# A two-layer decoder on one core: router by column tiles, two sequences in shared parts, and another order

## The chip, the core and the metric

The kernel runs on one core of a Trainium2 chip. Such a core has TensorE (matmuls and transposes, writing to PSUM), VectorE, ScalarE and GpSimd for the elementwise work, and SyncE, which issues nearly all transfers here; the five run side by side and meet at semaphores. The metric is the device time of one execution, in microseconds (us). Profiles name the engines PE, DVE, ACT, POOL and SP; PEld is TensorE's loading of weights.

## What is computed

Sixteen sequences of 128 tokens with 256 features go through six residual blocks, all in f32, with a context of the same shape for the two cross attentions:

```python
x = x + L0_attn(layernorm(x), qk, ov)                  # causal, one head of 256
x = x + L0_xattn(layernorm(x), ctx, ctx, mask, ...)    # 16 heads of 16
x = x + L0_ffn(layernorm(x), ...)                      # 1024 hidden, 4 of 16 blocks of 64 chosen by a router
x = x + L1_attn(layernorm(x), ...)                     # 16 heads, adds its own normalised input too
x = x + L1_xattn(layernorm(x), ctx, ctx, cell, ...)    # own layer norms, rotation, causal, equal cells
x = x + L1_ffn(layernorm(x), ...)                      # 8 experts of 128, the best 2, and a shared one of 256
```

The block FFN takes `softmax(x @ w_router + b_router)` and keeps a hidden block where it is among the four best. The expert FFN takes `sigmoid(x @ gate.T)`, keeps the two best experts, divides their scores by their sum and multiplies by 2.5:

```python
shared_out = swiglu(x, ws_gate, ws_up, ws_down)
topk_w, topk_idx = top_k(sigmoid(x @ gate_weight.T), 2)
combine = einsum("tk,tke->te", 2.5 * topk_w / (topk_w.sum(-1, keepdims=True) + 1e-20), one_hot(topk_idx, 8))
y = einsum("tei,ehi->teh", silu(g) * u, w_down)        # g, u: of every expert
out = einsum("te,teh->th", combine, y) + shared_out
```

## The kernel before

**Lanes.** Two sequences make a lane (`G = 2`, 256 tokens), so there are eight lanes (`NL`), whose x stays on the chip from the first load to the output. All work is written for one lane at a time. The expert FFN is dense: every lane goes through all eight experts, and a token's share of an expert it did not choose is zero.

**Steps of a lane.** `layer_0` (L1107) runs `causal_attention` (L677), `context_attention` (L730) and `block_ffn` (L762); `layer_1` (L1116) runs `self_attention` (L820) and `windowed_attention` (L855); `expert_ffn` (L964) follows by itself. Each normalises x (L343), transposes it on TensorE (`transposed`, L386, giving `srcT` with the tag `xT`) and multiplies. `attention` (L486) handles one sequence: scores for 16 heads in two score tiles (tag `s`, four PSUM banks), VectorE's row maxima `top`, a transpose `topT`, the maxima subtracted in `qs` on GpSimd, the scores once more the other way round, the exponentials `p` on ScalarE, and the products with the values `oT`, which use column tiles of the array: four tiles of 128 rows by 32 columns that work side by side. The scores use four row tiles of 32 rows. `unseen` holds masks, added to the scores by small bf16 matmuls (`hide`, L475).

**The parts that the change touches.** `router` (L621) multiplies with x as the stationary side and the router's 16 or 8 columns moving, for each sequence and half of the features; the logits stand in PSUM token by token, and for layer 0 VectorE adds the bias row. `values` (L441) projects one sequence into a bank, and VectorE adds the bias into the value tile `v`, then the other. `causal_attention` runs values, scores, softmax, transpose and product once for each sequence (`one`, L686). The sums of both FFNs (`y`) are made one sequence at a time, each in a bank of its own and added to x by VectorE. GpSimd adds the row biases to x, one sequence at a time. `rotate` (L652) fetches swapped rows through SyncE into the buffer `swap`, and GpSimd and VectorE combine them.

**The order.** It is written out by a planner, `Turns` (L65 to L240), at build time. The steps are generators; each `yield` names the engine of the next piece and the buffers it takes (`dict(bank=1)`), and `give` returns them. The planner keeps a time for each engine and each buffer from its own costs. `run` (L211) takes, among all threads whose buffers are there, the piece that can begin first, and among equals the one of lowest rank; the instructions of each engine are issued in that order, and nothing is reordered on the chip. A piece is never broken. `LIMITS` (L334) holds the number of buffers of each tag; `bank` are the four PSUM banks beside the scores'. Five lanes are in work at a time (`IN_FLIGHT`, L1121): layer 0 of lanes 0 to 7, then layer 1 of lanes 0 to 7, each begun when an earlier one ends (`more`, L1123). The expert weights come into the place of the block FFN's once the last layer 0 has ended (`late_weights`, L1096), and an expert FFN begins when a layer 1 is done, at most three beyond those ended.

Of the kernel before, what the change touches and what calls it, by code (L numbers as in the profile page):

```python
# [32 lines left out]


# [9 lines left out]
C_ALL = C_TRI8 + NE * NE  # L44
# [6 lines left out]
    ("L1_xattn_b_q", 2), ("L1_xattn_b_k", 2),  # L51
# [3 lines left out]
    ("L1_xattn_b_v", D), ("L1_xattn_b_o", D), ("L0_ffn_b_router", NB),  # L55
# [19 lines left out]

class Turns:
# [5 lines left out]

    HOP = 70.0
    HOP_FROM_PE = 200.0
    SWITCH = 91.0

# [21 lines left out]
    def give(self, tag, n=1):  # L108
        self.tiles[tag] += [self.now.at] * n
# [27 lines left out]
    def act(self, name, out, *args, **kw):  # L137
        self.charge(ACT, 200 + 0.8 * self.width(out, args))
        getattr(self.nc.scalar, name)(out, *args, **kw)  # L139
# [7 lines left out]
    def moved(self, n_bytes):  # L147

        self.moves = max(self.moves, self.now.at) + n_bytes / 300.0
        self.now.at = self.moves + 2000.0  # L150

# [59 lines left out]
    def run(self, more):  # L211

        while True:
            more()
            best = None
            for i, th in enumerate(self.threads):
# [13 lines left out]
                if ok and (best is None or (at, th.rank, i) < best[0]):  # L230
                    best = (at, th.rank, i), th
# [3 lines left out]
            (at, _, _), th = best  # L235
# [4 lines left out]
            th.at, th.last = max(th.at, at), engine  # L240
            self.resume(th, None)


class Thread:
    def __init__(self, gen, rank, at, parent):
        self.gen, self.rank, self.at, self.parent = gen, rank, at, parent
        self.last, self.ask, self.waits, self.children, self.result = None, None, 0, [], None
# [3 lines left out]
def decoder(ctx: ExitStack, tc: tile.TileContext, a: dict, out: bass.AP):  # L251
# [6 lines left out]
    ps_s = ctx.enter_context(tc.tile_pool(name="ps_s", bufs=2, space=PSUM))  # L258
    ps = ctx.enter_context(tc.tile_pool(name="ps", bufs=4, space=PSUM))

    dram = ctx.enter_context(tc.tile_pool(name="dram", bufs=1, space=bass.MemoryType.DRAM))
# [54 lines left out]

    scaled_bias = {
# [7 lines left out]
    v_tiles = [keep.tile([P, G, H * HA + CT - HA], F32, name=f"v{i}") for i in range(4)]  # L325
# [4 lines left out]
    for t in tops:  # L330
        nc.gpsimd.memset(t, 0.0)


    LIMITS = dict(  # L334
        bank=4, s=2, oT=1, xn=6, xT=5, qk=5, qs=3, kb=3, v=4, p=4, oS=2, on=4, hm=8, tmp=3, rank=2, selT=2, p0=2,
        pT0=2, unseen=4, chosen=3, swap=2, words=1, top=3,
# [77 lines left out]
    def project(w, at, xT, j):  # L414

        q.landed(w)
        t = bank([P, D], "pr")
        for d in range(DC):
            q.matmul(t, xT[:, d, j * S : (j + 1) * S], w[:, d, at : at + D], start=d == 0, stop=d == DC - 1)
        return t  # L420

# [19 lines left out]
    def values(w, at, xT, bias):  # L441
        yield PE, dict(v=1, bank=1)
        v = v_tiles.pop(0)
        for j in range(G):
            if j:
                yield PE, dict(bank=1)
            t = project(w, at, xT, j)
            yield DVE
            q.dve(
                "tensor_tensor",  # L450
                v[:, j, 0 : H * HA].rearrange("p (h e) -> p h e", e=HA)[:, :, 0:HD],
                t.rearrange("p (h e) -> p h e", e=HD),
                row(bias).rearrange("p (h e) -> p h e", e=HD),
                ALU.add,
            )
            q.give("bank")
        return v
# [28 lines left out]
    def attention(qT, kb, v, j, unseen=None, to=None):  # L486
# [7 lines left out]
        yield PE, dict(s=2)  # L494
        ss = banks()
# [11 lines left out]
        for t2, s in enumerate(ss):  # L507
# [4 lines left out]
            q.give("s")  # L512
        yield PE, dict(bank=1)
# [16 lines left out]
        yield PE, dict(s=2)  # L530
        ss = banks()
# [12 lines left out]
        def exponentials(s):  # L544
# [3 lines left out]
            q.give("s")  # L548
            return p

        pTs = yield [exponentials(s) for s in ss]
        yield PE, dict(oT=1, bank=1)

# [17 lines left out]
        q.give("bank")  # L571
        yield PE, dict(bank=1)
# [48 lines left out]
    def router(w, xT, n):  # L621
        yield PE, dict(bank=1)
        t = bank([P, G, n], "rt")
        for j in range(G):
            for d in range(DC):
                q.matmul(t[:, j, :], xT[:, d, j * S : (j + 1) * S], w[:, d, :], start=d == 0, stop=d == DC - 1)
        return t

    def output_projection(on, w, l, j, gain=None, bias=None, free=None):
# [16 lines left out]
        y = project(w, 0, oT, 0)  # L646
# [30 lines left out]
    def causal_attention(l):  # L677
# [8 lines left out]
        def one(j):  # L686
            js = slice(j * S, (j + 1) * S)
            yield PE, dict(bank=1)
            t = project(w["ov"], 0, xT, j)
            yield ACT, dict(on=1)  # L690
            v = new("on", [P, D], "v1")
            q.act("copy", v, t)
            q.give("bank")
            yield PE, dict(bank=1)
            s = bank([P, S], "s0")
            for d in range(DC):
                q.matmul(s, qT[:, d, js], xT[:, d, js], start=d == 0, stop=d == DC - 1)
            yield DVE, dict(p0=1)
            p = new("p0", [P, S], "p0")
            q.dve("tensor_tensor", p, s, causal, ALU.add)  # L700
            q.give("bank")
            m = small.tile([P, 1], F32, tag="m0", name="m0")
            q.dve("tensor_reduce", m, p, AX.X, ALU.max, negate=True)
            yield ACT
            total = small.tile([P, 1], F32, tag="total", name="total")
            q.act("activation", p, p, AF.Exp, bias=m, accum_out=total)
            yield PE, dict(bank=1)
            t = bank([P, S], "pt0")
            q.transpose(t, p, ident)
            q.give("p0")  # L710
            yield ACT, dict(pT0=1)
            pT = new("pT0", [P, S], "pT0")
            q.act("copy", pT, t)
            q.give("bank")
            yield PE, dict(bank=1)
            o = bank([P, D], "o0")
            q.matmul(o, pT, v, start=True, stop=True)
            q.give("pT0")
            q.give("on")
            yield DVE  # L720
            r = small.tile([P, 1], F32, tag="r0", name="r0")
            q.dve("reciprocal", r, total)
            q.dve("scalar_tensor_tensor", x[l][:, j, :], o, r, x[l][:, j, :], ALU.mult, ALU.add)
            q.give("bank")

        yield [one(j) for j in range(G)]
        q.give("xT")
        q.give("qk")

# [32 lines left out]
    def block_ffn(l):  # L762

        xT = yield from transposed((yield from normalise(x[l])))
        rt = yield from router(w["r0"], xT, NB)
        yield DVE, dict(chosen=1)
        pr = small.tile([P, G, NB], F32, tag="pr", name="pr")
        q.dve("tensor_tensor", pr, rt, row("L0_ffn_b_router").unsqueeze(1).to_broadcast([P, G, NB]), ALU.add)
# [15 lines left out]
        for j in range(G):  # L784
            q.pool("tensor_tensor", x[l][:, j, :], x[l][:, j, :], row("L0_ffn_b2"), ALU.add)
# [21 lines left out]
        for j in range(G):  # L807
            yield PE, dict(bank=1)
            y = bank([P, D], "y0")
            for f in range(8):  # L810
                q.matmul(
                    y, hm[f // 2][:, f % 2, j * S : (j + 1) * S], w["w2"][:, f, :], start=f == 0, stop=f == 7
                )
            if j == G - 1:
                q.give("hm", 4)
            yield DVE
            q.dve("tensor_tensor", x[l][:, j, :], x[l][:, j, :], y, ALU.add)
            q.give("bank")

    def self_attention(l):  # L820
# [4 lines left out]
        def residual():  # L825
            for j in range(G):

                yield POOL
# [408 lines left out]
```

## Time and profile before

| what | us |
|---|---|
| median of three runs | 850.48 (850.39 to 851.54) |
| the profiled execution | 849.42 |
| its span, first to last instruction | 847.4 |
| router matmuls, 128, by their records | 16.0 |
| `v` bias adds, VectorE, 48 | 20.1 (0.418 each) |
| `x<-x,y` adds, VectorE, 32 | 13.4 (0.418 each) |
| `x<-x,rows` adds, GpSimd, 32 | 23.6 (0.751 each) |

An f32 matmul appears as two matmul instructions. Matmuls are pipelined: a record of 0.38 us can be followed by the next start after 0.22. So a group's busy time is the union of its records, and what an instruction holds the array is read from the distance of two starts. The 40 slices of the span show who is busy when, in tenths:

```
PE   6999999999999999999979999999999999999998
DVE  5446565565262644546685686675566575555533
ACT  4555434362544354626747565565343424212111
POOL 5345454153165443636777875445422331100000
```

The one slice of TensorE below nine in the middle is the 21st, from 424 to 445 us. In the last nine slices ScalarE and GpSimd have little to do: only expert FFNs are left.

### The profile page before, as it was taken

Reading aid. Unit: us, or ns where it says so; the run is one execution under the profiler, and the core shown is the slowest. Engines: PE = TensorE matmul, PEld = TensorE weight load, DVE = VectorE, ACT = ScalarE, POOL = GpSimd, SP = SyncE. Lnnn points to the kernel's source line nnn. Section 1 sums busy time; section 2 is a strip of 40 time slices with the busy share of each in tenths; the row PEclk is TensorE's granted clock in tenths of the full one; section 3 lists DMA queues with packets and bytes.
Section 4 is the critical chain, followed back from the end, with each engine's and each line's share of the span. In section 5 each row is a group of like instructions: output and inputs, shape, how many; then the busy total and the mean of one; then the engine's idle time right before and its main releaser. Section 6 shows DMA issues by size and latency. Waiting matters only on the chain.

```text
span 847.4 us, 19890 instructions
## 1 busy us (share of the span) xinstructions
PE 818.3 (97%) x8128; PEld 661.2 (78%) x8128; DVE 481.7 (57%) x1218; ACT 372.1 (44%) x801; POOL 350.0 (41%) x606
## 2 busy tenths in 40 slices
PE   6999999999999999999979999999999999999998
PEld 5877678778787777876758867878778888888887
DVE  5446565565262644546685686675566575555533
ACT  4555434362544354626747565565343424212111
POOL 5345454153165443636777875445422331100000
PEclk9999999999999999999999999999999999999999
DMA  8325202112100000160120102010100100000000
GB/s 285 113 72 162 70 25 34 36 38 78 40 1 13 2 2 2 39 187 1 52 64 13 53 3 74 3 48 30 51 2 1 63 13 2 13 1 14 13 12 13
DMA packets 41178, 36.83 MB, mean 43 GB/s; under 512 B 6784, under 2 KB 36608, under 8 KB 40448
## 3 DMA queue, kind: packets, MB, share of 16 engines
q1 hardware_dynamic: 41088, 35.57, 13.8%
q8 instruction: 64, 1.05, 0.5%
q14 instruction: 26, 0.21, 0.1%
HBM read 27.16 MB, written 4.19 MB: 37 GB/s over the span
## 4 chain that ended last, share of the span: by engine, by line
PE 85%; DVE 6%; POOL 4%; ACT 2%; issue 2%; DMA 1%; SPq 0%; POOLq 0%; ACTq 0%; DVEq 0%
PE gu L126 16%; PE s L126 14%; PE y L126 14%; PE pj L126 11%; PE pr L126 9%; PE hp L126 7%; PE oT L126 5%; PE tps L131 3%; PE o L131 2%; PE rt L126 2%; DVE top L135 1%; POOL rstd L145 1%; DMA swap<-kT 1%; ACT p L139 1%; PE wb L126 1%
## 5 line engine op out<-in xcount | busy, mean ns | idle before, releaser
L135 DVE TENSOR_REDUCE top<-s 128x8 f32<-128x1024 f32 x96 | 112.8, 1217 | 31.1 <-PE s L126 31.0
L139 ACT ACTIVATE p<-s 128x1024 f32<-128x1024 f32 x96 | 94.6, 1027 | 60.0 <-PE s L126 60.0
L126 PE MATMUL gu<-srcT,gu 128*128 128x256 f32 x512 | 118.4, 380 | 1.5 <-DVE hm L135 0.9
L145 POOL TENSOR_TENSOR qs<-qT,less 128x512 f32<-128x512 f32 x48 | 61.0, 1272 | 112.1 <-ACT less L139 105.7
L126 PEld LDWEIGHTS gu<-srcT,gu 128*128 128x128 f32 x512 | 93.8, 190 | 16.8 <-DVE hm L135 1.2
L139 ACT ACTIVATE sg<-gu 128x256 f32<-128x256 f32 x80 | 30.8, 385 | 116.6 <-PE gu L126 111.2
L145 POOL TENSOR_SCALAR rstd<-mv 128x2 f32<-128x2 f32 x72 | 16.6, 230 | 121.0 <-DVE mv L135 116.6
L126 PE MATMUL hp<-srcT,L_w 128*128 128x256 f32 x256 | 65.9, 387 | 0.0
L126 PE MATMUL s<-qs,kb 32*128 32x128 f32 x1536 | 59.4, 286 | 5.7 <-POOL qs L145 2.9
L126 PEld LDWEIGHTS s<-qs,kb 32*128 32x128 f32 x1536 | 49.5, 188 | 16.9 <-issue 7.3
L126 PE MATMUL y<-L_w,hm 128*128 128x256 f32 x256 | 59.0, 383 | 0.0
L126 PE MATMUL y<-down,hm 128*128 128x256 f32 x256 | 58.4, 381 | 0.0
L145 POOL TENSOR_SCALAR kb<-kT,consts 128x256 f32<-128x256 f32 x96 | 53.1, 566 | 10.3 <-ACT kT L139 9.7
L126 PE MATMUL s<-kb,qT 32*128 32x256 f32 x768 | 56.5, 401 | 0.6 <-DVE top L135 0.6
L126 PE MATMUL oT<-p,v 128*32 128x128 f32 x1536 | 52.5, 276 | 2.1 <-ACT p L139 2.0
L135 DVE TENSOR_TENSOR x<-x,y 128x256 f32<-128x256 f32 x32 | 13.4, 418 | 71.4 <-PE y L126 71.4
L126 PEld LDWEIGHTS y<-L_w,hm 128*128 128x128 f32 x256 | 47.7, 190 | 8.0 <-issue 1.5
L145 POOL TENSOR_TENSOR rstd<-rstd,power 128x2 f32<-128x2 f32 x72 | 51.3, 713 | 6.0
L126 PEld LDWEIGHTS hp<-srcT,L_w 128*128 128x128 f32 x256 | 44.3, 190 | 11.5 <-issue 3.3
L126 PEld LDWEIGHTS y<-down,hm 128*128 128x128 f32 x256 | 47.8, 190 | 6.3 <-issue 0.2
L145 POOL TENSOR_TENSOR eq<-eq,consts 128x512 bf16<-128x512 bf16 (+1 forms) x16 | 15.0, 940 | 89.7 <-DVE eq L135 89.6
L135 DVE SCALAR_TENSOR_TENSOR sg<-sg,gu 128x256 f32<-128x256 f32 x80 | 33.2, 415 | 31.3 <-ACT sg L139 31.1
(149 smaller groups left out, 1625.1 us busy)
## 6 DMA issues: line engine op xcount, KB each, us to landing
unseen<-hidden SPq DMA_DIRECT2D x128, 64.0 KB, 2.4
c<-in_ctx SPq DMA_DIRECT2D x16, 256.0 KB, 3.0
x<-in_x SPq DMA_DIRECT2D x8, 256.0 KB, 6.3
L_w<-in_L_w SPq DMA_DIRECT2D x2, 1024.0 KB, 6.4
hidden<-plain SPq DMA_DIRECT2D x32, 64.0 KB, 1.5
gu<-in_L_gu SPq DMA_DIRECT2D x2, 1024.0 KB, 5.2
swap<-kT SPq DMA_DIRECT2D x16, 128.0 KB, 2.1
swap<-qT SPq DMA_DIRECT2D x16, 128.0 KB, 2.1
```

Source lines behind the costliest of these rows:

```text
L126: self.nc.tensor.matmul(out, lhsT, rhs, **kw)
L131: self.nc.tensor.transpose(out, src, ident)
L135: getattr(self.nc.vector, name)(out, *args, **kw)
L139: getattr(self.nc.scalar, name)(out, *args, **kw)
L145: getattr(self.nc.gpsimd, name)(out, *args, **kw)
```

## The change

The file also gets code that sorts tokens by expert and runs only the chosen ones (`routing`, `shared`, `plan`, `expert_tile`, `combining`, `blank`). It is reached for lanes named in `GROUPS`, and that is empty, so all lanes take `expert_ffn` as before; of that code there remain a few small constant tables (33 more columns of `consts`, two 128x128 tiles made once by VectorE).

The router makes four products, one for each sequence and half of the features, in the four column tiles, with the router's columns padded to 32 as the stationary side and x moving. ScalarE copies the result (with the bias, in layer 0), TensorE transposes it once, and VectorE adds the two halves:

```diff
+    def router(w, xT, n, bias=None):
         yield PE, dict(bank=1)
-        t = bank([P, G, n], "rt")
+        t = bank([P, S], "rT")
         for j in range(G):
             for d in range(DC):
-                q.matmul(t[:, j, :], xT[:, d, j * S : (j + 1) * S], w[:, d, :], start=d == 0, stop=d == DC - 1)
-        return t
+                c = j * DC + d
+                q.matmul(
+                    t[c * CT : (c + 1) * CT, :], w[:, d, :], xT[:, d, j * S : (j + 1) * S], start=True, stop=True
+                )
+        yield ACT, dict(p0=1)
+        sb = new("p0", [P, S], "rT")
+        if bias is None:
+            q.act("copy", sb, t)
+        else:
+            q.act("activation", sb, t, AF.Identity, bias=col(bias, 0))
+        q.give("bank")
+        yield PE, dict(bank=1)
+        t = bank([P, G * DC, CT], "rt")
+        q.transpose(t.rearrange("p c n -> p (c n)"), sb, ident)
+        q.give("p0")
+        return t.rearrange("p (g d) n -> p g n d", d=DC)[:, :, 0:n]
...
-        q.dve("tensor_tensor", pr, rt, row("L0_ffn_b_router").unsqueeze(1).to_broadcast([P, G, NB]), ALU.add)
+        q.dve("tensor_reduce", pr, rt, AX.X, ALU.add)
...
-        yield ACT
-        sc = small.tile([P, G, NE], F32, tag="sc", name="sc")
-        q.act("activation", sc, rt, AF.Exp, scale=-1.0)
-        q.give("bank")
+        yield DVE
+        sc = small.tile([P, G, NE], F32, tag="sc", name="sc")
+        q.dve("tensor_reduce", sc, rt, AX.X, ALU.add)
+        q.give("bank")
+        yield ACT
+        q.act("activation", sc, sc, AF.Exp, scale=-1.0)
```

`values`, the FFN sums and causal attention put both sequences into one bank, and one instruction of VectorE or ScalarE takes them out; in causal attention the exponentials and the last scaling stay one for each sequence. GpSimd's bias adds cover both sequences too.

```diff
+    def products(parts):
+        y = bank([P, G, D], "y")
+        for j in range(G):
+            pairs = parts(slice(j * S, (j + 1) * S))
+            for i, (a, b) in enumerate(pairs):
+                q.matmul(y[:, j], a, b, start=i == 0, stop=i == len(pairs) - 1)
+        return y
...
-        for j in range(G):
-            yield PE, dict(bank=1)
-            y = bank([P, D], "y0")
...
-            yield DVE
-            q.dve("tensor_tensor", x[l][:, j, :], x[l][:, j, :], y, ALU.add)
-            q.give("bank")
+        yield PE, dict(bank=1)
+        y = products(lambda js: [(hm[f // 2][:, f % 2, js], w["w2"][:, f, :]) for f in range(8)])
+        q.give("hm", 4)
+        yield DVE
+        q.dve("tensor_tensor", x[l], x[l], y, ALU.add)
+        q.give("bank")
```

The order: a thread that holds score tiles, or asks for them, is treated as if it could begin 200 ns earlier; `holds` is set ahead of each pass over the scores and cleared after the maxima, and after the copy `oS`. The planner's cost of a ScalarE instruction with a bias or scale of its own per row grows by 80 ns each. The turns and buffers change, and the limit of three on begun experts goes:

```diff
+    LEAD = 200.0
...
-                if ok and (best is None or (at, th.rank, i) < best[0]):
-                    best = (at, th.rank, i), th
+                first = th.holds or "s" in takes
+                key = (max(at - self.LEAD * first, self.free_at[engine] - first), not first, th.rank, i)
+                if ok and (best is None or key < best[0]):
+                    best = key, th, at
...
-        bank=4, s=2, oT=1, xn=6, xT=5, qk=5, qs=3, kb=3, v=4, p=4, oS=2, on=4, hm=8, tmp=3, rank=2, selT=2, p0=2,
-        pT0=2, unseen=4, chosen=3, swap=2, words=1, top=3,
+        bank=4, s=2, oT=1, xn=6, xT=4, qk=5, qs=3, kb=3, v=3, p=4, oS=2, on=4, xe=1, hm=8, tmp=3,
+        rank=2, selT=2, p0=2, pT0=1, unseen=4, chosen=3, swap=1, words=1, top=3,
...
+    TURN = [(0, l) for l in range(7)]
+    for l in range(NL):
+        TURN += [(1, l), (0, l + 7)] if l + 7 < NL else [(1, l)]
...
-        if n < 2 * NL and n - len(ended) < IN_FLIGHT and (n < NL or n - NL in ended[:NL]):
+        if n < 2 * NL and n - len(ended) < IN_FLIGHT and (TURN[n][0] == 0 or (0, TURN[n][1]) in ended):
...
-        if ready and experts_begun[0] < min(len(ended) - NL, experts_ended[0] + 3):
-            l = ended[NL + experts_begun[0]]
+        dense = [l for k, l in ended if k and l not in group_of]
+        if ready and experts_begun[0] < len(dense):
+            l = dense[experts_begun[0]]
```

So the turns are layer 0 of lanes 0 to 6, layer 1 of lane 0, layer 0 of lane 7, layer 1 of lanes 1 to 7.

## The prediction

> **What bounds the kernel now.** I read the page first: who is busy, and what the chain of waits runs through.
>
> ```profile
> PE 818.3 (97%) x8128; PEld 661.2 (78%) x8128; DVE 481.7 (57%) x1218; ACT 372.1 (44%) x801; POOL 350.0 (41%) x606
> ...
> PE 85%; DVE 6%; POOL 4%; ACT 2%; issue 2%; DMA 1%; SPq 0%; POOLq 0%; ACTq 0%; DVEq 0%
> ```
>
> TensorE is busy in 97% of the span and carries 85% of the chain; nobody else is above 57%. So a step counts here only if it takes TensorE's time, or makes TensorE wait. A matmul's recorded end is modelled, so I used its starts instead: from one instruction's start to the next.
>
> ```profile
> 103.86 0.96 PE L126 MATMUL rt<-L_router,srcT 128*128 128x16 f32 x8
> 104.67 0.63 PE L131 MATMUL o<-consts,oS 128*128 128x128 f32 x4
> ...
> 100.80 1.08 PE L126 MATMUL oT<-p,v 128*32 128x128 f32 x32
> 101.81 0.48 PE L126 MATMUL hp<-srcT,L_w 128*128 128x256 f32 x1
> ```
>
> In the timeline of TensorE (start, length, and how many), a router's eight instructions hold the array from 103.86 to 104.67, 0.81 us; the 32 column-tiled ones of one attention from 100.80 to 101.81, 1.01 us. (An f32 matmul is two instructions, so the counts are twice the matmuls of the code.) Taking every kind at its usual distance (0.216 us for 128x256 f32, 0.109 for a transpose and so on) and adding up all 8128, TensorE needs 761 us of work. It changes between whole-array and tiled shapes 330 times; each costs 0.09 us, seen as 1.82 us in place of 1.73 for eight projection instructions that a tiled one follows: 30 us. It first starts at 6.2 us, and 3.8 us come after its last start. 847.4 - 761 - 30 - 6.2 - 3.8 leaves 46 us of real waits. That is all that an order can win.
>
> Where they lie, by the view of stretches (time, TensorE busy):
>
> ```profile
> 100.00:350.00 250.00, 247.03 (x2455) 198.62 (x2454) 129.32 (x308) 109.64 (x238) 108.54 (x174) 1.00 0.09 23
> 350.00:525.00 175.00, 164.87 (x2131) 129.17 (x2130) 112.02 (x260) 103.95 (x210) 113.04 (x191) 0.99 0.19 57
> 425.00:450.00 25.00, 19.64 (x314) 14.56 (x312) 18.64 (x39) 13.39 (x27) 19.07 (x28) 0.93 0.17 50
> 525.00:665.00 140.00, 137.67 (x1550) 110.23 (x1549) 87.63 (x216) 69.04 (x143) 57.73 (x98) 1.00 0.08 24
> 665.00:844.00 179.00, 178.37 (x1074) 151.35 (x1072) 97.30 (x287) 37.73 (x94) 20.99 (x38) 1.00 0.04 14
> ```
>
> By starts, the 46 us are: 9.5 up to 100 us (loads and a cold pipeline), 9.6 from 100 to 350, 19.9 from 350 to 525, 5 from 525 to 665, 2 after that. The thick part is 350 to 525, and its reason is in the lists of FFN and expert work: the last block-FFN sum ends at 366.0, the first expert matmul is this:
>
> ```profile
> 522.49 1.03 PE L126 MATMUL pr<-L_qkv,srcT 128*128 128x256 f32 x4
> 523.35 1.03 PE L126 MATMUL gu<-srcT,gu 128*128 128x256 f32 x4
> ```
>
> For 157 us there is only attention, whose chain goes over five engines, and no long FFN work to put between. After 665 us there is nothing to win: experts run back to back.
>
> **The router** (L621). Removed: eight instructions, 0.81 us. Added: eight of the column-tiled form, a quarter of the attention's (1.01 less the way out of the tiled shape, 0.13, is 0.88; a quarter 0.22), 0.09 into the tiled shape, 0.13 out, and one transpose of 0.11: 0.55. Saved 0.26 in each of 16 routers: 4.2 us. Bounds: a router that lies beside other tiled work pays no change of shape (0.33, saved 7.7); one whose transpose finds its copy late pays a start of 0.1 more (saved 2.6). Beside it ScalarE gets 16 copies (0.46 by the row of a 128x128 activation with a column bias, 0.28 by that of a plain copy: 5.9 us in all), and VectorE eight small reductions more (0.18 by `mr`, 1.5 us); the other eight stand for the bias add of 0.19. Both engines have over 40% free, so nothing on the path. The router itself answers some 1 us later (copy, two hops, transpose); the other four lanes hide this, and in the tail a router runs one expert ahead (that at 728.29 belongs to the expert whose matmuls start near 761.8). Behind the waiting copy stand other lanes' exponentials, which give the score banks back; a copy that finds its matmuls late holds them by the 0.2 us of a hop. Without cover it is 16 x 1 = 16 us. The wider router tables add under 0.1 MB of loads, behind which only later lanes' x wait: nothing.
>
> **Shared parts.** TensorE's matmuls stay the same in number and size in values (L441), causal attention (L677) and both sums. What changes is the pieces: values lose 24 of 48, causal attention 32 of 64, the sums 16 of 32, 72 pieces fewer, each of which could find its semaphore late. Pieces of kind `pr` have 6.4 us of waits in 78 groups, 0.08 each; for 72 pieces that would be 5.9, yet most of it lies in a few long waits that stay. I take 2 us, bounds 0 and 5.9. VectorE's adds become half as many: 0.42 for 256 columns, 0.68 (the shortest 128x512 row, `swap`) to 0.85 (its mean) for 512; GpSimd's bias adds 0.75 against 1.27. Both engines gain a little, which is off the path, but at the very end it is not:
>
> ```profile
> 842.88 1.03 PE L126 MATMUL y<-L_shared,hm 128*128 128x256 f32 x4
> 843.95 0.42 DVE L135 TENSOR_TENSOR x<-x,y 128x256 f32<-128x256 f32 x1 [3.90 <-PE y L126]
> 844.40 0.37 SPq L1035 DMA_DIRECT2D out_x<-x  x1
> ```
>
> The last add is now of 512 columns: 0.3 us later (0.26 to 0.43). What stands behind it is the output's DMA alone.
>
> [...] Today the first sequence's add at 839.63 runs while TensorE sums the second in another bank. [...]
>
> **The order.** Four things in it. (a) Layer 1 of lane 0 is begun before layer 0 of lane 7. Begins follow ends, and the ends stand one turn apart (sums end at 205.4 and 237.2), so layer 1 begins some 32 us earlier, and the last block FFN ends as much later: the stage without FFN shrinks from 157 to about 93 us. Its waits above the rate of 100 to 350 (1 us in 25) are 19.9 - 7 = 12.9; times 93/157 is 7.6: saved 5 us. Bounds: nothing, and all 12.9. (b) Threads that hold a score bank go first, and TensorE may be kept free up to 0.2 us for them. That is at most 144 pieces x 0.2 = 29 us of new waits, and at most the 16 us that now lie ahead of scores, masks and values on TensorE as a gain; the first needs every piece to use its whole lead, so I take 0 with bounds -10 and +10. (c) Fewer buffers: xT 5 to 4, v 4 to 3, swap 2 to 1. One swap buffer was held from its DMA at 423.45 to the GpSimd add's end at 438.9, 15.4 us; sixteen of these are 246 us in the 313 from 367 to 680. One buffer is just enough, so rotations will queue; SyncE has `unseen` and `c` loads behind them, and attention waits for these. I take 2 us, bounds 0 and 19 (below). (d) The limit on experts begun falls; `hm` holds one at a time anyway (5 of 8): nothing.
>
> **The sum.** -4.2 - 2 + 0.3 - 5 + 0 + 2 = -8.9 us: the span goes from 847.4 to 838.5. The profiled execution took 849.42, 2.0 over its span, and the median shown is 850.48, 1.1 over that; adding 3.1 gives **841.6 us**. With the small bounds about it, 832 to 848.
>
> **Rivals.** *The order brings nothing:* the stage without FFN stays as it is because the first expert isn't held up by its turn. For this: lane 0's layer 1 is done at 432, yet the expert's router runs at 478.7, so buffers, not the turn, cost the last 90 us. Then -4.2 + 0.3 = -3.9: 846.6. *Starved of buffers (the other side):* one xT and one v less stop two lanes at a time in the stage that already lives on attention alone. If all of 350 to 525 waits like 400 to 450 does (11.1 us in 50), it is 3.5 x 11.1 = 39 against 19.9, 19 us more; with the router's gain and the tail 847.4 + 19 - 3.9 = 862.5, and 865.6 as a median. It decides as soon as new waits exceed what is sure, 4.2 + 2 - 0.3 = 5.9, by 1.7. Against: `kb` stays at 3, which held three lanes in attention already, and experts with 180 us of work stand behind. *The change doesn't do what it says:* the new sorted-experts code is not reached, as its list of groups is empty; the router's saving may be given back through its second wait. Then 850.
>
> **How the numbers follow.** Forecast 0.56; no gain by order 0.14; starved 0.24; nothing 0.06. 0.2% of 850.48 is 1.7 us, about what a measurement can tell from none. Faster (below 848.8): 0.54 + 0.10 = 0.64; within: 0.09, the rest of the second case and the fourth; slower: 0.27, the starved case and a tail of the forecast. Of the range, 830 to 861, the low end is the forecast less half of what the low bounds could add (3.5 + 3.9 + 7.9 + 10 = 25 us), for they won't all be met; the high end reaches into the starved case, short of its full price.
>
> **What would show it.** The eight `rt` instructions followed by a copy and a transpose, 0.55 us of array time in place of 0.81; `v` adds 24 of about 0.7 us; the first `gu` near 490 us and the last block-FFN sum near 398; TensorE's busy share above 95% in 400 to 450. It would be wrong if the stage without FFN keeps its 157 us, if `swap` DMAs or `srcT` come to stand in the chain, or if short gaps of up to 0.2 us appear ahead of `s` and `oT` everywhere.

## The result, and the profile after

| | before | after |
|---|---|---|
| median of 9 runs, us | 850.56 | 847.84 |
| after / before | | 0.9971 [0.9961, 0.9982] |
| profiled execution, us | 849.42 | 847.23 |
| its span, us | 847.4 | 845.4 |
| TensorE's work / changes of shape / waits, us | 759.7 / 30.4 / 47.4 | 752.3 / 32.5 / 50.7 |

The change gains 0.29%: the kernel is faster, as forecast, by 2.7 us and not by 8.9. The last row of the table is the prediction's account by starts, taken again for both traces with one table of usual distances (before's work comes to 759.7 us this way, 761 in the prediction). What TensorE loses while its clock is granted at half (0.50 in 632 to 637 us of the changed kernel) counts as waits here: by the mean granted clock, 1.7 us before (0.998) and 3.4 after (0.996). TensorE has 7.4 us less to do and waits 3.3 us more, 1.7 of them by the clock. The page after, by its lines of busy time and of the chain:

```profile
PE 816.1 (97%) x8144; PEld 650.9 (77%) x8144; DVE 474.4 (56%) x1165; ACT 372.9 (44%) x801; POOL 343.1 (41%) x573
...
PE 89%; DVE 3%; POOL 3%; ACT 3%; issue 1%; DMA 0%; ACTq 0%; POOLq 0%
```

The bound is the same. VectorE is at 56% in place of 57, GpSimd at 41% as before. The stretches of before again (time, TensorE busy, ...; the third column from the right is the granted clock), with 600 to 660 us added:

```profile
100.00:350.00 250.00, 246.96 (x2572) 195.53 (x2567) 130.03 (x299) 117.82 (x253) 114.10 (x181) 1.00 0.11 29
350.00:525.00 175.00, 169.25 (x2111) 131.70 (x2109) 111.38 (x243) 104.36 (x211) 105.55 (x165) 1.00 0.15 49
425.00:450.00 25.00, 24.65 (x280) 18.93 (x272) 19.39 (x38) 17.91 (x40) 14.46 (x25) 1.00 0.07 23
525.00:665.00 140.00, 131.14 (x1414) 102.03 (x1407) 84.71 (x225) 63.05 (x133) 60.94 (x102) 0.98 0.09 27
600.00:660.00 60.00, 52.88 (x439) 40.88 (x439) 34.24 (x100) 21.85 (x49) 12.92 (x32) 0.94 0.02 5
665.00:844.00 179.00, 176.33 (x1065) 147.31 (x1063) 94.43 (x267) 36.04 (x92) 15.79 (x26) 1.00 0.04 14
```

The thin stretch of before, 350 to 525, is filled (169.25 against 164.87, and 24.65 of 25 in place of 19.64 in 425 to 450). A new one has opened: in 600 to 660 TensorE is busy for 52.88 of 60 us, where before had this:

```profile
600.00:660.00 60.00, 59.12 (x683) 47.61 (x684) 37.81 (x105) 25.85 (x53) 16.85 (x34) 1.00 0.08 23
```

That is where the gain went. Waits by starts, in us, by stage:

| stage | before | after |
|---|---|---|
| 0 to 100 | 9.5 | 6.6 |
| 100 to 350 | 10.2 | 10.4 |
| 350 to 525 | 20.0 | 14.0 |
| 525 to 600 | 2.4 | 4.7 |
| 600 to 660 | 2.6 | 13.0 |
| after 660 | 2.8 | 1.9 |

The timeline of TensorE inside the new stall:

```profile
628.48 0.65 PE L140 MATMUL tps<-consts,xn 128*128 128x128 f32 x4 [0.45 <-DVE hm L144]
629.79 0.44 PE L140 MATMUL ot<-consts,xn 128*128 128x128 f32 x2 [0.66 <-DVE hm L144]
630.67 0.66 PE L140 MATMUL ot<-consts,xn 128*128 128x128 f32 x2 [0.44 <-DVE hm L144]
...
632.06 3.78 PE L135 MATMUL pr<-L_xo,oT 128*128 128x256 f32 x8 [0.52 <-DVE hm L144]
...
641.34 1.99 PE L135 MATMUL gu<-srcT,L_shared 128*128 128x256 f32 x8 [0.52 <-DVE hm L144]
...
643.96 1.99 PE L135 MATMUL gu<-srcT,L_shared 128*128 128x256 f32 x8 [0.52 <-DVE hm L144]
...
646.35 0.43 PE L135 MATMUL rT<-srcT,L_router 128*32 128x128 f32 x8 [0.28 <-DVE sc L144]
```

Between the gate matmuls of one expert there is little else than that expert's own short steps, each a gap of half a microsecond behind a product of VectorE. The last lanes' attention, which filled these gaps elsewhere, is missing. What it lacks is seen on ScalarE, where the pairs of `gained` copies stand (the normalised input that the windowed attention's projections read; a pair fills one tile):

```profile
628.11 1.01 ACT L149 ACTIVATE gained<-tps,cols 128x256 f32<-128x256 f32 x2
647.00 1.02 ACT L149 ACTIVATE gained<-tps,cols 128x256 f32<-128x256 f32 x2
658.94 1.02 ACT L149 ACTIVATE gained<-tps,cols 128x256 f32<-128x256 f32 x2
```

`gained` and `srcT` come from the same four `xT` buffers. Each begun expert takes one for its `srcT` ahead of its router and keeps it to its last gate matmul (`expert_ffn`). Experts' routers run at 589.95, 598.05 and 646.35; by the written order, the copies behind them are these:

```profile
472.60 0.58 ACT L149 COPY srcT<-tps 128x512 f32<-128x512 f32 x1
...
591.66 0.63 ACT L149 COPY srcT<-tps 128x512 f32<-128x512 f32 x1
...
598.78 0.65 ACT L149 COPY srcT<-tps 128x512 f32<-128x512 f32 x1
```

The first of them is held until 645.9, where the row of 643.96 ends. So three of the four buffers are with experts, and one is left for the last windowed attention, which must have the inputs of its keys and of its values both before its first projection (`of_context`). One pair is copied at 628.11. The next stands transposed in its PSUM bank, without a place to be copied to, until 647.00, the third until 658.94, while one expert works alone.

### The profile page after: what moved, and what is told of

Same layout as the page of the kernel before. It is cut to its first block, busy times and chain, and to the rows that moved or that the text cites. A ratio compares the mean times of both kernels' runs of the same rounds, so it can differ in the third digit from the quotient of the medians.

```text
span 845.4 us, 19813 instructions
## 1 busy us (share of the span) xinstructions
PE 816.1 (97%) x8144; PEld 650.9 (77%) x8144; DVE 474.4 (56%) x1165; ACT 372.9 (44%) x801; POOL 343.1 (41%) x573
## 3 DMA queue, kind: packets, MB, share of 16 engines
q1 hardware_dynamic: 41088, 35.62, 13.7%
## 4 chain that ended last, share of the span: by engine, by line
PE 89%; DVE 3%; POOL 3%; ACT 3%; issue 1%; DMA 0%; ACTq 0%; POOLq 0%
PE s L135 16%; PE gu L135 16%; PE y L135 14%; PE pj L135 12%; PE pr L135 10%; PE hp L135 7%; PE oT L135 5%; PE tps L140 3%; PE o L140 3%; POOL rstd L155 1%; PE topT L140 1%; PE o L135 1%; PE wb L135 1%; ACT p L149 1%; PE ot L140 1%
## 5 line engine op out<-in xcount | busy, mean ns | idle before, releaser
L149 ACT ACTIVATE sg<-gu 128x256 f32<-128x256 f32 x80 | 30.7, 384 | 145.4 <-PE gu L135 145.2
L135 PE MATMUL y<-L_w,hm 128*128 128x256 f32 x256 | 56.9, 380 | 0.0
L135 PEld LDWEIGHTS oT<-p,v 128*32 128x32 f32 x1536 | 39.1, 109 | 13.8 <-issue 8.0
L135 PEld LDWEIGHTS s<-kb,qT 32*128 32x128 f32 x768 | 36.1, 184 | 16.2 <-issue 6.9
```

The source lines that it names most:

```text
L135: self.nc.tensor.matmul(out, lhsT, rhs, **kw)
```

## Experiments

Except where the order is said to be frozen, a kernel's order is planned anew. In the expectations, the *planner's own end* is the time at which the planner, by its own table of costs, sees the last instruction begin. All twelve in one table (waits by starts, in us, of the profiled execution, and its span):

| run | median | ratio to before [95%] | waits | 0–100 | 100–350 | 350–525 | 525–600 | 600–660 | 660+ | planner's end | span |
|---|---|---|---|---|---|---|---|---|---|---|---|
| before | 850.6 | | 47.4 | 9.5 | 10.2 | 20.0 | 2.4 | 2.6 | 2.8 | 817.3 | 847.4 |
| after | 847.84 | 0.9971 [0.9961, 0.9982] | 50.7 | 6.6 | 10.4 | 14.0 | 4.7 | 13.0 | 1.9 | 814.8 | 845.4 |
| e1_xT5 | 850.36 | 0.9995 [0.9985, 1.0004] | 55.4 | 6.5 | 10.2 | 23.4 | 9.0 | 3.7 | 2.6 | 818.8 | 849.4 |
| e2_limit2 | 868.48 | 1.0215 [1.0198, 1.0232] | 70.8 | 6.1 | 10.4 | 14.0 | 4.8 | 8.5 | 27.1 | 833.7 | 865.6 |
| e3_buffers | 868.35 | 1.021 [1.0195, 1.0225] | 73.5 | 14.6 | 15.3 | 12.5 | 3.7 | 20.9 | 6.4 | 824.2 | 867.8 |
| e4_nolead | 878.53 | 1.0336 [1.03, 1.0372] | 88.3 | 10.4 | 13.4 | 36.3 | 5.0 | 16.8 | 6.4 | 838.4 | 881.5 |
| f1_old_router | 854.26 | 1.0042 [1.0025, 1.0059] | 51.2 | 6.2 | 10.4 | 14.0 | 4.4 | 12.7 | 3.5 | frozen | 851.5 |
| f2_xT5_late | 840.43 | 0.988 [0.9861, 0.9898] | 44.5 | 6.2 | 10.4 | 13.7 | 4.7 | 7.6 | 2.0 | 810.6 | 839.2 |
| f3_xT5_frozen | 847.43 | 0.9951 [0.9932, 0.997] | 50.5 | 7.4 | 10.4 | 15.1 | 4.8 | 10.9 | 1.9 | frozen | 845.4 |
| g1_xT5_from300 | 839.73 | 0.9878 [0.9858, 0.9898] | 42.7 | 7.3 | 10.4 | 16.4 | 5.0 | 1.8 | 1.9 | 807.1 | 837.7 |
| h1_old_turns | 865.76 | 1.0173 [1.0156, 1.019] | 71.3 | 7.4 | 16.5 | 29.0 | 8.0 | 4.4 | 6.0 | 829.2 | 865.4 |
| h2_no_lead | 845.06 | 0.9946 [0.9927, 0.9966] | 52.4 | 6.9 | 12.2 | 20.1 | 4.4 | 6.4 | 2.3 | 815.6 | 847.0 |
| h3_other_constants | 841.47 | 0.989 [0.9875, 0.9905] | 43.5 | 6.6 | 8.6 | 16.5 | 5.9 | 3.5 | 2.4 | 806.7 | 838.7 |
| h4_hop72 | 871.51 | 1.0248 [1.0226, 1.0269] | 77.4 | 8.9 | 18.4 | 24.4 | 9.7 | 3.8 | 12.1 | 839.9 | 872.3 |

TensorE's work is 752.3 us in all of them but f1 (759.7), and the changes of shape cost 30.4 to 32.8: the spans differ by waits. Time lost by the clock is among these: by the mean granted clock of the execution, 12 us in e2_limit2 and h1_old_turns (0.986), 17 in e4_nolead (0.981), 21 in e3_buffers (0.976), 9 in h4_hop72 (0.990), and none in g1_xT5_from300 and h3_other_constants (1.000).

### Parts of the order undone one at a time

Theory A: the new order's parts have each their price, and the shortage of `xT` at the end costs what the turns gain. Theory B, the rival: the greedy planner's result is a draw (which of many orders comes out turns on accidents of the planner's costs), and any edit draws again. First, each suspected part was taken back alone:

```diff
# e1_xT5
-        bank=4, s=2, oT=1, xn=6, xT=4, qk=5, qs=3, kb=3, v=3, ...
+        bank=4, s=2, oT=1, xn=6, xT=5, qk=5, qs=3, kb=3, v=3, ...
# e2_limit2 (and the counter that it needs)
-        if ready and experts_begun[0] < len(dense):
+        if ready and experts_begun[0] < min(len(dense), experts_ended[0] + 2):
# e3_buffers (and a fourth `v` tile made at the start)
-        ... xT=4, ... v=3, ... swap=1, ...
+        ... xT=5, ... v=4, ... swap=2, ...
# e4_nolead
-                first = th.holds or "s" in takes
+                first = False
```

> The changed kernel with five xT buffers in place of four; nothing else, though the planner then writes another order. Theory A (four xT buffers, three of them held by expert FFNs that were begun early, stop the last windowed attention between 610 and 660 us, and it holds two of the four PSUM banks meanwhile): that stall goes, some 7 us of idle TensorE and 3.5 us of half clock; time 847.8 - 8 = 840, at most 844, and the two `gained` pairs of one lane follow each other at once. Theory B (any new order moves the time by some us either way, and the buffers are no cause): somewhere in 843 to 852, and lanes of expert and window work still lock somewhere. Theory C (priority for score holders brings the waits): 847 to 848, no change.

> The changed kernel with four xT buffers, but an expert FFN is begun only while fewer than two are begun and not ended. Theory A: experts hold at most two xT, so the last windows get theirs; stall at 610 to 660 us smaller, 840 to 845; experts' FFNs start about as early as before. Theory B: 843 to 852. Theory C: 847 to 848.

> The changed kernel with all buffers as they were before the change (xT 5, v 4, swap 2). Theory A: as with five xT or a little better, 837 to 842, since v and swap matter little by it. If the swap buffer or v was the cause in place of xT, this is clearly faster than five xT alone, by 3 us or more. Theory B: 843 to 852.

> The changed kernel without the precedence of threads that hold or ask for score tiles (their 200 ns of lead and the tie-break are off); buffers and turns as in the change. Theory A: the precedence is about neutral, 845 to 851, and the lock of window and experts on xT is still there. Theory C: short waits ahead of scores and `oT` fall and the time with them, 840 to 844. If the precedence was the gain of the change: 850 to 856.

None of them is faster than the changed kernel; three are 20 to 31 us slower, outside every range that was named for them. In e1_xT5 the stretches show that the stall in question did go, and that another one came:

```profile
350.00:525.00 175.00, 164.13 (x1932) 126.93 (x1925) 111.42 (x246) 101.01 (x207) 105.01 (x170) 0.99 0.14 47
600.00:660.00 60.00, 58.22 (x620) 46.52 (x619) 34.31 (x91) 28.26 (x60) 20.37 (x40) 1.00 0.09 28
```

TensorE is busy 58.22 of 60 us in the last attention, in place of 52.88, but 164.13 in place of 169.25 between 350 and 525: waits of 3.7 and 23.4 us against 13.0 and 14.0. More buffers let lanes start at other moments, from the first lanes on, and the planner takes other turnings. In e2_limit2 TensorE's order is the changed kernel's up to 564 us, and so are the waits of the stages up to 600. The want of `xT` is gone there, with four buffers: the last three pairs of `gained` copies follow each other.

```profile
626.34 1.00 ACT L149 ACTIVATE gained<-tps,cols 128x256 f32<-128x256 f32 x2
628.80 1.03 ACT L149 ACTIVATE gained<-tps,cols 128x256 f32<-128x256 f32 x2
630.41 1.06 ACT L149 ACTIVATE gained<-tps,cols 128x256 f32<-128x256 f32 x2
```

From 630 to 660 us TensorE is busy for 29.94 of 30 us; the 8.5 us of waits lie ahead of that. So begun experts are what keeps the buffers from the attention. What costs the kernel its 868.48 us comes after 660: the next expert is begun only when one has ended, its transposes, router and choice then have nobody beside them, and TensorE stands idle for 2.57, 3.54 and 5.43 us at 697, 761 and 826 us and runs at half clock for 6.8 us behind each of these (a granted clock of 0.95 over 660 to 864 us). So the time of a replanned kernel tells little of one part's price: it must be read where the waits lie, or the edit must be kept from disturbing what lies ahead of it, or the order must be frozen.

### The router alone, in a frozen order

The changed kernel's order was written down as a list and replayed, with the old router's eight matmuls in the place of the transpose and the old bias add in that of the reduction (a plain copy by VectorE for the experts' scores). ScalarE's copies fall away, and nothing else moves in any queue.

```diff
# f1_old_router
-        q.transpose(t.rearrange("p c n -> p (c n)"), sb, ident)
+        for j in range(G):
+            for d in range(DC):
+                q.matmul(t[:, j, :], xT[:, d, j * S : (j + 1) * S], w[:, d, 0:n], start=d == 0, stop=d == DC - 1)
...
-        q.dve("tensor_reduce", pr, rt, AX.X, ALU.add)
+        q.dve("tensor_tensor", pr, rt, row("L0_ffn_b_router").unsqueeze(1).to_broadcast([P, G, NB]), ALU.add)
```

> The changed kernel with its order frozen (the planner replays the choices it made for the changed kernel) and the router's old matmuls: eight instructions in the place of the transpose, the bias added by VectorE, no copy; the slots of the first matmuls and of the copy are empty. Theory A (the router's gain is real, and it was eaten by waits of the new order): TensorE's work at the usual distances rises from 752 to 760 us, changes of shape fall by some 30, and the time rises by 4 to 6 us to 852 to 854. Theory D (the router's second wait costs as much as its matmuls save): 846 to 849, no change.

854.26 against 847.84 us: the new router is worth 6.4 us at this order, or 6.0 by the two ratios to before. By starts, 7.4 of work, less 2.1 for 23 more changes of shape, 0.5 of waits and 0.2 of a later first start make 6.0 of the spans' 6.1 us. The timelines of TensorE show one router of f1_old_router, then one of the changed kernel:

```profile
349.61 0.96 PE L171 MATMUL rt<-L_router,srcT 128*128 128x16 f32 x8
350.43 1.97 PE L171 MATMUL pj<-gained,L_xk 128*128 128x256 f32 x8
```

```profile
344.02 0.43 PE L135 MATMUL rT<-srcT,L_router 128*32 128x128 f32 x8
344.38 1.99 PE L135 MATMUL pj<-srcT,L_qkv 128*128 128x256 f32 x8
...
347.90 0.27 PE L140 MATMUL rt<-consts,rT 128*128 128x128 f32 x1
348.01 1.25 PE L135 MATMUL pj<-gained,L_xk 128*128 128x256 f32 x5
```

From start to start 0.82 us against 0.36 + 0.11 = 0.47; with the 0.09 into the tiled shape where its neighbour is not tiled that makes 0.56. The transpose stands 3.5 us behind its matmuls, with other lanes' work between: the second wait that the router got is covered.

### The stall at 600 us alone

The fifth `xT` buffer is given back, but the planner may use it only from a set time of its plan on; before that its plan is the changed kernel's. Then the memory alone, with the changed kernel's order replayed as it is.

```diff
# f2_xT5_late (g1_xT5_from300: 300000.0)
-        bank=4, s=2, oT=1, xn=6, xT=4, qk=5, qs=3, kb=3, v=3, ...
+        bank=4, s=2, oT=1, xn=6, xT=5, qk=5, qs=3, kb=3, v=3, ...
...
+    q.tiles["xT"][0] = 600000.0
# f3_xT5_frozen
-        return work.tile(shape, dtype, tag=tag, name=name, bufs=LIMITS[tag])
+        return work.tile(shape, dtype, tag=tag, name=name, bufs=LIMITS[tag] + (tag == "xT"))
```

> The changed kernel with a fifth xT buffer that the planner may use only late in its plan, so that the order of TensorE is that of the changed kernel up to about 628 us and free after it. Theory A2 (the lock of 600 to 660 us is xT, and the five-buffer kernel lost by another order ahead of it): waits between 600 and 660 us fall from 13 to about 4, and the time to 838 to 842. Theory B2 (the stall of that stage is that of the work left, not of a buffer): waits stay at 10 to 13 us there, or come back after 660, and the time is 845 to 849.

> The changed kernel with its whole order frozen, and five xT buffers in the memory where the planner counted four. Nothing stands elsewhere in any queue, but an instruction that waited for an xT buffer's readers waits no longer. If the chip waits on the buffer itself: 840 to 845. If the order, once written, holds each instruction back behind its neighbours (theory A2 and B2 alike): 847 to 849, no change.

> The changed kernel with the fifth xT buffer usable from 300 us of the plan on: the order of the first third is kept, and the rest is drawn anew with the buffer. Theory A2: the lock is gone and the first stages are as before, 836 to 843. If every new order is a draw of its own: anywhere from 840 to 865, and its waits lie in another stage.

f2_xT5_late takes 840.43 us, 7.4 less than the changed kernel. TensorE runs the same order in both up to 632 us; ScalarE's copies part at the second pair:

```profile
627.52 1.01 ACT L149 ACTIVATE gained<-tps,cols 128x256 f32<-128x256 f32 x2
629.05 1.00 ACT L149 ACTIVATE gained<-tps,cols 128x256 f32<-128x256 f32 x2
634.74 1.02 ACT L149 ACTIVATE gained<-tps,cols 128x256 f32<-128x256 f32 x2
```

The second pair comes at 629.05 in place of 647.00, the third at 634.74 in place of 658.94. The waits of 600 to 660 fall from 13.0 to 7.6 (4 had been expected), and no other stage gains by more than 0.4. A plan drawn anew from 600 us on without the buffer was not run, so a part of the 7.4 us may be a better draw behind 632; that the copies come 18 and 24 us sooner is the buffer. f3_xT5_frozen stays at 847.43 with the stall in place (10.9): the memory is no help where the written order has the copy behind the expert. With the buffer usable from 300 us of the plan on, g1_xT5_from300 has nearly no stall left, at 839.73 us, the fastest kernel of this study; its stretches:

```profile
350.00:525.00 175.00, 167.85 (x2076) 130.56 (x2078) 116.99 (x257) 101.57 (x207) 107.37 (x166) 1.00 0.15 50
...
600.00:660.00 60.00, 57.49 (x430) 47.93 (x431) 32.81 (x92) 22.41 (x52) 18.67 (x36) 1.00 0.08 27
```

57.49 of 60 us, with the full clock (1.00 in place of 0.94).

### Is the order a draw?

Three edits of g1_xT5_from300 and one of the changed kernel: two parts of the order taken back, and two changes of constants that alter no rule, buffer or instruction (h3_other_constants halves the lead, though, which the change itself brought).

```diff
# h1_old_turns
-    TURN = [(0, l) for l in range(7)]
-    for l in range(NL):
-        TURN += [(1, l), (0, l + 7)] if l + 7 < NL else [(1, l)]
+    TURN = [(0, l) for l in range(NL)] + [(1, l) for l in range(NL)]
# h2_no_lead
-    LEAD = 200.0
+    LEAD = 0.0
# h3_other_constants
-    LEAD = 200.0
+    LEAD = 100.0
-    HOP_FROM_PE = 200.0
+    HOP_FROM_PE = 190.0
-    SWITCH = 91.0
+    SWITCH = 80.0
-        self.charge(ACT, 200 + 0.8 * self.width(out, args) + 80 * by_row)
+        self.charge(ACT, 200 + 0.8 * self.width(out, args) + 100 * by_row)
# h4_hop72, on the changed kernel
-    HOP = 70.0
+    HOP = 72.0
```

> The kernel of g1_xT5_from300 (839.73 us) with one part of the order taken back: layer 0 of all eight lanes first, then layer 1 of all eight, as before the change. TensorE's work stays at 752.3 us. Theory A (the turns are worth what the stage without FFN gets shorter by): the first gu comes some 30 us later against the last hp, the waits of 350 to 525 us rise from 16.4 to about 22, the time is 844 to 848. Theory B (every new order is a draw, and the turns are one input of it among many): the waits grow by more than this and not in that stage alone; the planner's own end is 22 us later, so 855 to 865. Theory C (turns are worth nothing): 838 to 842.

> The kernel of g1_xT5_from300 with the 0.2 us of lead set to 0: threads that hold or ask for score tiles still go first among equals, but TensorE is never kept free for them. Work unchanged. Forecast's step (b): 0 with bounds of 10 us to both sides, so 839.7 give or take 10; the page would show it as waits of 42.7 us give or take 10. Theory B (draw of an order): a change of any sign that the planner's own end foretells, here 8.5 us later, so 845 to 852. Theory of a real precedence: TensorE's waits rise in 350 to 525 us, where scores, masks and values are the work, and not elsewhere.

> The kernel of g1_xT5_from300, planned with four constants a little different: lead 100 ns in place of 200, a hop from TensorE 190 in place of 200, a change of shape 80 in place of 91, 100 more for a ScalarE instruction with its own row bias in place of 80. No work changes. The planner's own end is 0.4 us earlier than g1's. If its estimate can order plans this near to each other: 839 to 840. If the plan's last us are lost by what the planner doesn't price: anything from 837 to 848, and never below the 833 us that work, shape changes, first start, tail and the waits of the first 350 us leave.

> The changed kernel (847.84 us) planned with a hop between engines of 72 ns in place of 70: nothing of the work, the buffers, the turns or the precedence changes. Theory A (the order's quality comes from its rules and buffers): a 3% change of one constant leaves the time within some 3 us, 845 to 851. Theory B (the greedy order is a draw whatever the edit): the planner's own end is 25 us later than the changed kernel's, and the chip would show 865 to 875, the growth all in TensorE's waits, with 752.3 us of work.

h4_hop72 speaks for theory B: 2 ns more for a hop in the planner's costs, and the kernel takes 871.51 us, 23.7 more than the changed kernel, all of it in waits (77.4 against 50.7 in the profiled executions), spread over every stage but 600 to 660. The page of h4_hop72:

```profile
PE 831.3 (95%) x8144; PEld 659.7 (76%) x8144; DVE 482.5 (55%) x1165; ACT 374.8 (43%) x801; POOL 343.6 (39%) x573
```

The same 8144 matmuls, 95% of a longer span. h3_other_constants, the other neutral edit, is 1.7 us slower than g1, a draw of nearly the same worth. (The floor of 833 us that was named for it doesn't follow from its terms, which add up to some 813.) Against this scatter h2_no_lead (5.3 us slower than g1, 9.7 more waits, 3.7 of them in 350 to 525 and 4.6 in 600 to 660) tells nothing certain of the lead; the 3.7 are even less than the 5.1 us that this execution lost at half clock between 362 and 373 us (0.97 over the 175 us). h1_old_turns is 26.0 us slower than g1, about as much as a neutral edit did. Its stretches:

```profile
100.00:350.00 250.00, 245.49 (x2445) 196.26 (x2443) 122.95 (x288) 113.11 (x244) 106.13 (x163) 0.98 0.10 27
350.00:525.00 175.00, 161.16 (x2059) 122.83 (x2061) 97.09 (x220) 98.72 (x196) 106.27 (x168) 0.96 0.14 46
```

From the last `hp` (block FFN) to the first `gu` (expert) it is 166 us (373 to 539) against 106 (383 to 489) in g1: the stage without FFN grows as the turns foretell. TensorE's busy time in 350 to 525 falls by 6.7 us, its waits rise by 12.6, some 7 of these by the clock (0.96 of 175 us). But h4_hop72 added 10.4 us of waits in the same stage with the turns untouched, so the place doesn't show that the turns did it. The rest, 16.0, lies in other stages, where the forecast saw no price for the turns.

The table's last columns show what the draw can be read from: the span is 28.6 to 32.4 us above the planner's own end in nine of the twelve orders that were planned, 36.2 in h1_old_turns, and 43.1 to 43.6 in e3_buffers and e4_nolead, the two executions with the lowest granted clock. A plan's end sorts good draws from bad ones; it doesn't resolve the last few us.

## Why the prediction was right and wrong

**The router: right, a little too small.** The sum had -4.2 us in bounds of -7.7 to -2.6. TensorE's account gives -7.4 + 2.1 = -5.3, and f1_old_router 6.0 to 6.4 in time. The new router takes the 0.55 us that were forecast where it pays both changes of shape; the 16 of them pay 2.1 us for changes in place of 16 x 0.22 = 3.5, because some stand beside other tiled work. As forecast, its later answer is hidden.

**Shared parts: right in sign, not tried alone.** The value adds are 24 of 512 columns at 0.69 us, in the groups by line:

```profile
L144 DVE TENSOR_TENSOR v<-pr,rows 128x512 f32<-128x512 f32 x24 | 16.5, 686 | 25.2 <-PE pr L135 25.0
```

The waits of kind `pr` went from 6.4 to 4.0 us, where 2 were forecast as saved; the order changed too, so what the sharing did of this is open. At the end the add and the output's DMA stand as forecast:

```profile
841.73 0.69 DVE L144 TENSOR_TENSOR x<-x,y 128x512 f32<-128x512 f32 x1 [7.34 <-PE y L135]
```

0.69 us in place of 0.42, and the tail behind TensorE's last start grew from 3.8 to 4.1: the +0.3 of the sum. No run adds the first sequence's half while TensorE still sums the second in the same bank, so whether the end could have stayed where it was is open.

**Order (a), the turns: met in place and size, not shown as the cause.** The prediction let the stage without FFN shrink from 157 to about 93 us, with the first expert near 490 and 5 us saved. TensorE's timeline has the last block-FFN sum and the first expert at

```profile
389.63 2.32 PE L135 MATMUL y<-L_w,hm 128*128 128x256 f32 x10
...
473.27 1.89 PE L135 MATMUL gu<-srcT,gu 128*128 128x256 f32 x8
```

so 81 us; waits fell by 6.0 in 350 to 525 and by 2.9 ahead of 100. TensorE is busy for 99% of 400 to 450. So the size is met, but after h4_hop72 it can't be claimed for the turns alone, and h1_old_turns doesn't part them from a draw.

**Order (c), fewer buffers: the step that failed.** The sum had +2 us for the buffers, with all of its range for the attention between 350 and 525 and for `swap`. It looked in the wrong place and at the wrong holder. A begun expert takes an `xT` ahead of its router and keeps it to its last gate matmul (472.60 to 645.9 for one of them), long before it gets `hm`. With four in place of five, the last attention was left with one `xT` at 600 to 660 us, a stage to which the prediction had given 5 us of waits from 525 to 665 and no risk; its rival of starved buffers named `xT` too, but for 350 to 525. The cost is 7.4 us by f2_xT5_late and 8.1 by g1_xT5_from300, draws included: about 6 more than the term had, which is the size of the miss (847.84 against 841.6). Without the stall the kernel takes 840.43 or 839.73, near to the forecast. The term's upper bound, 19, did cover it.

**Order (d), no limit on begun experts: the reason was wrong, the price is open.** The sum had "nothing", because `hm` holds one expert at a time. `hm` does bound the experts' work, but not what begun experts keep from others, as e2_limit2 shows: with two of them, the attention had its `xT` in time. The old limit was three, though, and three is what stood there: the first expert had ended (its sum is added at 587.69), and three more would have been allowed. So in this stage the old limit would have let the same three hold their buffers, and the lost fifth buffer made the difference. That is worked out from the code and the trace; the old limit was not run.

**Order (b), precedence: taken as 0, and open.** Without it h2_no_lead was 5.3 us slower than g1, and e4_nolead 30.7 slower than the changed kernel: the first well within, the second a little beyond what a neutral edit did (23.7). The short gaps ahead of `s` and `oT` everywhere that would have spoken against it did not come: TensorE's idle time ahead of `s` fell from 6.3 to 1.9 us, and that ahead of `oT` rose from 2.1 to 3.8, of which 1.87 is one gap ahead of 612.44.

**What no step held.** The prediction took an order's change as a sum of mechanisms with prices of a few us each. On this kernel a plan made anew, with no reason to be different at all, moved the time by 23.7 us (h4_hop72). So the chance of 0.27 for slower had too little under it: a bad draw was no rival there, only a starved buffer was. That the measured 847.84 came as near to 841.6 as it did is in part this draw's luck: h4_hop72, the same change, took 871.51.

## What to carry to other kernels

Where a greedy planner writes the order, a change's parts can't be priced by replanning without each: freeze the order and swap the part, or let the edit act only after a set time, and compare with an edit that should do nothing. When a buffer is taken away, ask for every holder how early it takes it and how late it gives it back, above all for work that has been begun and waits for something else; the buffer that bounds its work (`hm`) need not be the one that it keeps from others (`xT`). Try several neutral constants and keep the best plan: of the two tried here one moved the time by 23.7 us, the other by 1.7; the router's change brought 6.

## What the runs showed of the hardware

The stall of TensorE cost more than its gaps. Three stretches of the changed kernel (time, TensorE busy, ...; the clock is the third from the right):

```profile
628.00:632.00 4.00, 1.99 (x10) 1.04 (x9) 2.75 (x7) 3.15 (x8) 0.92 (x3) 0.81 0.02 4
632.00:637.00 5.00, 4.64 (x11) 3.14 (x12) 1.42 (x5) 0.18 (x1) 0.00 (x0) 0.50 0.00 0
...
641.00:646.00 5.00, 4.15 (x18) 3.12 (x18) 2.21 (x6) 0.53 (x3) 0.00 (x0) 1.00 0.00 0
```

In the first 4 us TensorE was half busy, with no single gap of over 0.66 us; within them, at 630.5, the granted clock fell to half (0.81 over the 4 us), and there it stayed for 6.8 us, to 637.3. The eight matmuls at 632.06 took 3.78 us, those at 641.34 took 1.99. Over the whole span the granted clock was 0.996, which is 3.4 us of the 845.4, behind some 2 us of gaps; in g1_xT5_from300 it was 1.000.

The same gaps need not cost this. f3_xT5_frozen runs the same instructions on TensorE in the same order, with the same gaps of 0.45, 0.66, 0.44 and 0.52 us, and kept the full clock there; its eight matmuls behind them, at 634.14, took 1.99 us:

```profile
600.00:660.00 60.00, 52.66 (x481) 40.64 (x482) 36.10 (x111) 23.50 (x54) 12.92 (x32) 1.00 0.02 5
```

Nor did the lower busy share go with the fall. In the 2.5 us ahead of the fall, 628.0 to 630.5, TensorE was busy for 1.12, all of that with transposes. From 610.0 to 612.5 us of the same trace it was busy for 0.63 of 2.5, with one gap of 1.87, and the full clock stayed (1.00). What took the clock down in the one and not in the other, the runs don't show.
